# An LSTM with its Wx sums as filler work: steps 16 to 31 by the pair scheme, with factors taken from where they are made

## The chip, the core and the metric

The kernel runs on one core of a Trainium2 chip. Its engines work in parallel, each in the order of its own instruction list: TensorE (PE, matmuls), VectorE (DVE), ScalarE (ACT), GpSimd (POOL) and SyncE (SP), which here only issues transfers. The metric is the device time of one execution in microseconds, the median of several runs. The profile is of one execution; its span is shorter than that execution's time by what lies before the first and behind the last instruction.

## What is computed

The reference is an LSTM over 512 time steps with a residual: batch 32, input and hidden size 512, all in float32.

```
xW = einsum('ntd,dg->ntg', x, Wx) + b
def step((h, c), xw_t):
    a = xw_t + h @ Wh                       # 4 x 512 columns: i, f, o, g
    i, f, o = sigmoid(...);  g = tanh(...)
    c = f * c + i * g
    h = o * tanh(c)
out = x + hs
```

The steps depend on each other. xW of a step depends on nothing but x and Wx, and has to be there before that step.

## The kernel before

**Two kinds of work on TensorE.** For every step k, h_part (L881) multiplies the transposed h by Wh: 32 matmuls onto PSUM banks that already hold xW of that step. Then the cell (L912 to L930) goes through ACT (sigmoid, tanh) and DVE (f·c, i·g, their sum, o·tanh c, the transpose to ht). While TensorE would wait for ht, it does filler work: a part of the Wx sums of later steps. The program is written out window by window: window v holds step k = v − OFF, and whatever products, sums and transfers the tables put there. Windows below OFF have no step, only the Wx sums with which step 0 can start.

**The Wx sums.** x is taken in rows of 8 steps. xW of a row goes by one of these ways:

- *Units* (UNITS, L91): one row and one quarter j of the columns, 7 products of Strassen's kind (s = 1 to 7), each over two blocks k: 56 matmuls of 128x32 by 128x256 a unit, four units a row. A job is one unit; it begins in window job.w and its products are spread over five windows by products(v) (L590): s1, s5 and s6 early, s7 two windows later, s2 and s3 three, s4 four.
- *The pair scheme* (PAIR, L267): two rows together by 14 outer products of 28 matmuls each, with sums of x blocks ("nodes", L512, and s0 to s3, L540 to L543) on the left side, sums of Wx blocks ("factors") on the right, and sums of the results afterwards (L760, L776).
- *The cycle scheme* (CYCLE): four rows by 26 outer products, thirteen times; it begins at window START and carries steps 48 to 495. The last two rows go by units and by direct products.

PAIR_ROW = 4: rows 0 to 3 (steps 0 to 31) are 16 units, rows 4 and 5 (steps 32 to 47) one pair. OFF is 11, so that step 0 stands in window 11.

**What a product leaves.** The first products of a job add up in an "acc" bank, s5 in "p". ACT copies them out (copy_first, copy_fifth, L633 to L639), DVE adds acc and p to pu (L620, "pu_n" for job n), ACT puts pu and acc into the "pp" banks (L627, L628), and DVE adds acc and p again into pp (L629). On these sums the later products pile up: s7 overwrites acc and so waits for L620 of its job; s4 adds into the bank that L629 fills. evacuate(v) (L606) writes these out for one window.

**Factors.** A factor is four strips of Wx sums, of 256, 512, 512 and 512 columns, in two tiles from rings: wa (3 buffers) with the A part (768 columns) and wb (4 buffers) with the B part (1024). push_factors (L405) queues all of them as DVE additions (L418) to be done where there is room; keep (L384) stores each in DRAM by SP, and fetch (L1133) loads the factor that a product needs two windows ahead, also by SP. t_pair (L355, the lines L358 to L360) and t_sums make the sums of Wx blocks (tt_sb) on DVE from which units and factors are formed.

**Other engines.** ACT seeds the step's PSUM banks with xW (L870, L876) and fills xw with the bias (L843). POOL loads xW of step k + 3 from DRAM with an adding transfer (load_xw, L847), and adds x to h for the output (L988): one 128x128 sum a step. SP loads Wh (load_wh, L352, four transfers), rows of x (load_row, L317), the residual rows, and stores xW (L659), factors and output.

Of the kernel before, what the change touches and what calls it, by code (L numbers as in the profile page):

```python
# [14 lines left out]
P = 128  # L15
B = 32
# [52 lines left out]
FACTORS_FROM = 6  # L69
# [20 lines left out]
PAIR_ROW = 4  # L90
# [77 lines left out]
PAIR_SPAN = 18  # L168
START = PAIR_AT + PAIR_SPAN
START_STEP = HEAD - LEAD  # L170
OFF = START - START_STEP
# [3 lines left out]
def pair_begin(n):  # L175

    return n + n * (PAIR_SPAN - PAIRS) // PAIRS

# [14 lines left out]
LOAD_AT = (4, 10, 12)  # L193
WH_AT = (2, 3, 4, 5)
# [62 lines left out]
class Run:  # L257
# [20 lines left out]
def kernel(  # L278
# [124 lines left out]
    factors_left = []  # L403

    def push_factors():  # L405
        v = nc.vector
        made, ops, done = {}, [], []

        def source(u, part):
            if u < 8:  # L410
                return parts_of(u)[part]
            a, b = made[u - 8]
            return (a[:, 0:1], a[:, 1:3], b[:, 0:2], b[:, 2:4])[part]

        def outer(n, how, a, b, part):
            if n not in made:
                made[n] = ring(n, f"make_{n}")
            (v.tensor_add if how == "add" else v.tensor_sub)(source(8 + n, part), source(a, part), source(b, part))  # L418

        for op in B_OPS:  # L420
            if isinstance(op, int):
                n = -1 - op
                ops.append((0, lambda n=n: keep(n, made[n])))
            else:
                for part, columns in enumerate((C, 2 * C, 2 * C, 2 * C)):
                    ops.append((columns, lambda op=op, part=part: outer(*op, part)))
        for n in range(R):
            if streamed(n) and len(B_OF[n]) == 1:
                ops.append((0, lambda i=B_OF[n][0][0], n=n: keep(n, parts_of(i))))
        for i, (columns, fn) in enumerate(ops):  # L430

            def go(fn=fn, i=i):
                fn()
                done.append(fn)
                factors_left.append(len(ops) - 1 - i)

            at = FACTORS_FROM + min(i / 5, 5 + (i - 25) / 12)
            push(at, columns, go, lambda v, i=i, at=at: len(done) == i and v >= at - 1)


# [149 lines left out]
    def products(v):  # L590
        for late, ss in ((4, (4,)), (2, (7,)), (0, (1,)), (1, (6,)), (0, (5,)), (1, (5,)), (3, (2, 3))):
            job = jobs.get(v - late)
            for s in ss if job and job.w < LATE_AT[0] else ():
                if job.w < EARLY and s not in (4, 7):
                    continue
                if s != 5 or job.w5 == v:
                    product(job, s)
                if s == 4:
                    job.release()
        for late, parts in enumerate(LATE_PLAN):  # L600
            job = jobs.get(v - late)
            for s, part in parts if job and job.w >= LATE_AT[0] else ():
                product(job, s, part)
                given[0] += 1

    def evacuate(v, room):  # L606
        taken = run_due(v - 0.5, FIRST_SUMS if room else 0)
        for half, late in ((1, 5), (0, 4)):
            job = jobs.get(v - late)
            if job:  # L610
                taken += job.finish(half)
# [7 lines left out]
        if job and job.w >= EARLY:  # L619
            nc.vector.tensor_add(job.pu[:, 1], job.acc, job.p5)  # L620
            taken += C + FIXED
        job = jobs.get(v - 3)
        if job:
            if room:
                taken += run_due(v, min(room - taken, BETWEEN))
            if job.w >= EARLY:
                nc.scalar.copy(job.pp[0], job.pu)  # L627
            nc.scalar.copy(job.pp[1][:, 0], job.acc)  # L628
            nc.vector.tensor_add(job.pp[1][:, 1], job.acc, job.p5)  # L629
            taken += C + FIXED  # L630
        return taken
# [13 lines left out]
    unit_free = spare + [pair.rearrange("p m t e b -> p m (t e b)") for pair in node_pairs[3:]]  # L645
    others = [t for i in range(8) if i not in RESIDENT for t in (raw[i], tt_[i])]

    def head_done():
        free.extend(t.rearrange("p (h n) c -> p h (n c)", h=2) for t in others)
        free.extend(spare)  # L650
        free.extend(spool.tile([P, 2, 2 * C], F32, name=f"slot_h{i}", tag="sums", bufs=2) for i in range(2))
        node_free.extend(pair[:, e] for pair in node_pairs[3:] for e in range(2))
# [52 lines left out]
    def slot(sb, v):  # L705
        ends = last_use(sb, v)
        if ends:
            sums[sb, v] = sums[sb, ends[0]]
            moved.add((sb, ends[0]))
        else:  # L710
            sums[sb, v] = free.pop(0)
        left_uses[sb, v] = sb.scheme.uses[v]

    def used(sb, v):
        if (sb, v) in left_uses:
            left_uses[sb, v] -= 1
            if left_uses[sb, v] == 0:
                f = sums.pop((sb, v))
                if (sb, v) not in moved:
                    free.append(f)  # L720
# [19 lines left out]
    def finish_product(job, sb, n):  # L740
        c = sb.scheme

        def finish(half):
# [24 lines left out]
            for v in c.by_ready[n]:  # L768
# [4 lines left out]
                def go(v=v):  # L773
# [12 lines left out]
                    and (last_use(sb, v) or len(free) > (at < sb.at + c.limit[v] - 0.5)),  # L786
# [31 lines left out]
    tail_banks = accs[(LATE_AT[0] + 1) % 2], pps[(2 * (len(UNITS) + PAIRS + R * NSB) + 2) % 3]  # L818
# [59 lines left out]
    state = {"c": c_init, "ht": h_init}  # L878
# [236 lines left out]
    def describe(job, sb, n):  # L1115
# [4 lines left out]
        job.kept = None if n < RAW_FIRST and sb.scheme is PAIR else kept.get(factor)  # L1120
        if job.kept is None:
# [11 lines left out]
    def fetch(v):  # L1133

        job = jobs.get(v + 2)
        if job and LATE_AT[0] > job.w >= PAIR_AT and job.kept:
            job.ring = [rpool.tile([P, 3, C], F32, name=f"wa_{job.w}", tag="wa", bufs=3), None]
# [15 lines left out]
        if v in WH_AT:  # L1153
            load_wh(WH_AT.index(v))
# [5 lines left out]
    with tc.manual_schedule():  # L1160
# [45 lines left out]
        for v in range(EARLY, OFF):  # L1206
            if v == NJ + 1:
                push_factors()
# [8 lines left out]
            evacuate(v, 0)  # L1217
# [13 lines left out]
        for k in range(T):  # L1231
# [77 lines left out]
```

## Time and profile before

| What | Value |
|---|---|
| median of 3 runs | 3077.12 us (3077.05 to 3077.36) |
| the profiled execution | 3077.34 us |
| its span | 3075.5 us |
| TensorE busy | 3067.8 us in 56,680 records |
| VectorE, ScalarE, GpSimd busy | 2277.3, 1993.6 and 815.0 us |
| granted TensorE clock | 1.00 |

A float32 matmul of the program leaves two records in the profile, so a product of 4 or 8 matmuls is 8 or 16 records. PE is the matmul, PEld the loading of its weights, which runs beside it. A row of the timeline gives start, duration, engine, line, operation, output and inputs, and in brackets how long the engine had been idle and what ended that. Durations of operations that follow each other overlap a little; the distance from start to start is what one costs in a queue. Line numbers are those of the kernel before.

### The profile page before, as it was taken

The page shows a single profiled execution, that of the slowest core. Times are in us where ns is not written, and L with a number is a line of the kernel's source. Part 1 is how long each engine was busy: PE and PEld are TensorE (multiplying, and loading weights), DVE is VectorE, ACT ScalarE, POOL GpSimd, SP SyncE. Part 2 cuts the span into 40 slices and gives each one's busy share as a digit, 9 for nine tenths or more (in the row PEclk, how much of TensorE's full clock was granted, in tenths as well). Part 3 has the DMA queues.
Part 4 walks back from the last instruction along what each step waited for, and adds up shares of the span by engine and source line. Part 5 has one row for each costly group of instructions (what it writes and reads, how often), then busy time and mean ns, then how long its engine had stood idle before and what let it go on. Part 6 is the DMA issues. An engine that isn't in the chain of part 4 may idle for free.

```text
span 3075.5 us, 133929 instructions
## 1 busy us (share of the span) xinstructions
PE 3067.8 (100%) x56680; PEld 2024.6 (66%) x56680; DVE 2277.3 (74%) x6441; ACT 1993.6 (65%) x5754; POOL 815.0 (26%) x1021
## 2 busy tenths in 40 slices
PE   9999999999999999999999999999999999999999
PEld 5566666666666666666666666666666666666666
DVE  5766777777777777777777777777777777777754
ACT  4566666666666666666666666766666666666665
POOL 0222222222222222222222222222222222222331
PEclk9999999999999999999999999999999999999999
DMA  8988898888889889898988988889898898988753
GB/s 298 301 258 216 228 254 218 254 227 237 241 212 266 226 240 241 211 265 212 261 222 216 270 219 250 226 219 263 218 260 224 227 256 219 258 225 220 196 118 72
DMA packets 343527, 710.71 MB, mean 231 GB/s; under 512 B 45456, under 2 KB 111504, under 8 KB 342416
## 3 DMA queue, kind: packets, MB, share of 16 engines
q1 hardware_dynamic: 269344, 568.41, 56.2%
q0 software_dynamic: 73152, 133.20, 27.2%
q8 instruction: 446, 7.31, 1.0%
q14 instruction: 153, 1.25, 0.1%
q10 hardware_dynamic: 432, 0.53, 0.1%
HBM read 515.97 MB, written 185.99 MB: 228 GB/s over the span
## 4 chain that ended last, share of the span: by engine, by line
PE 99%; DVE 1%; DMA 0%; ACT 0%; issue 0%; SPq 0%; DVEq 0%
PE gates L885 53%; PE acc L581 18%; PE pp L581 18%; PE p L581 6%; PE gates L899 4%; PE pp L802 0%; PE acc L802 0%; DMA raw_sb<-in_L_cond_Wx_dram 0%; PE gates L581 0%; DVE raw_sb L776 0%; DVE c L952 0%; DVE fc L956 0%; DVE fc L950 0%; DVE ht L960 0%; DVE nodes L366 0%
## 5 line engine op out<-in xcount | busy, mean ns | idle before, releaser
L885 PE MATMUL gates<-wh_sb,ht 128*32 128x384 f32 (+1 forms) x30144 | 1725.5, 379 | 0.0
L885 PEld LDWEIGHTS gates<-wh_sb,ht 128*32 128x32 f32 x30144 | 1045.7, 110 | 681.9 <-issue 607.0
L988 POOL TENSOR_TENSOR oc<-xr,ht 128x128 f32<-128x128 f32 x509 | 383.0, 752 | 2162.0 <-DVE ht L930 1959.3
L847 POOL DMA_DIRECT2D xw<-xw x508 | 446.7, 880 | 82.0 <-DMA xw<-nodes 54.4
L922 ACT ACTIVATE s<-gates 128x256 f32<-128x256 f32 x472 | 181.3, 384 | 350.4 <-PE gates L885 339.3
L843 ACT COPY xw<-bias_sb 128x512 f32<-128x512 f32 x508 | 320.9, 632 | 2.0 <-DVE bias_sb L1210 2.0
L581 PE MATMUL pp<-wb,nodes 128*32 128x256 f32 x3920 | 314.7, 379 | 0.0
L925 DVE TENSOR_TENSOR fc<-s,c 128x128 f32<-128x128 f32 x471 | 137.0, 291 | 186.1 <-ACT s L922 183.1
L627 ACT COPY pp<-pu 128x512 f32<-128x512 f32 x398 | 240.0, 603 | 52.7 <-DVE tt_sb L760 21.5
L629 DVE TENSOR_TENSOR pp<-acc,p 128x256 f32<-128x256 f32 x400 | 170.9, 427 | 136.9 <-ACT pp L628 136.7
L929 DVE TENSOR_TENSOR fc<-s,ig 128x128 f32<-128x128 f32 x472 | 137.8, 292 | 177.5 <-ACT ig L928 177.5
L924 ACT ACTIVATE s<-gates 128x128 f32<-128x128 f32 x472 | 131.0, 278 | 147.2 <-PE gates L885 147.2
L870 ACT COPY gates<-xw 128x384 f32<-128x384 f32 x472 | 223.2, 473 | 3.8 <-DMA xw<-xw 3.6
L581 PE MATMUL pp<-wb,s 128*32 128x256 f32 x2656 | 213.2, 379 | 0.0
L581 PE MATMUL acc<-wb,s 128*32 128x256 f32 x2656 | 213.2, 379 | 0.0
L581 PE MATMUL p<-wa,s 128*32 128x256 f32 x2656 | 213.2, 379 | 0.0
L581 PE MATMUL acc<-wa,s 128*32 128x256 f32 x2656 | 213.2, 379 | 0.0
L928 ACT ACTIVATE ig<-c 128x128 f32<-128x128 f32 x472 | 146.3, 310 | 99.3 <-DVE c L927 60.8
L628 ACT COPY pp<-acc 128x256 f32<-128x256 f32 x400 | 144.9, 362 | 87.0 <-DVE tt_sb L760 35.3
L620 DVE TENSOR_TENSOR pu<-acc,p 128x256 f32<-128x256 f32 x398 | 165.2, 415 | 36.8 <-ACT p L639 35.6
L930 DVE STREAM_TRANSPOSE ht<-fc 128x128 f32<-128x128 f32 x472 | 147.0, 312 | 50.7 <-DVE fc L929 1.8
L639 ACT COPY p<-p 128x256 f32<-128x256 f32 x400 | 152.0, 380 | 38.9 <-PE p L581 36.6
(284 smaller groups left out, 4528.3 us busy)
## 6 DMA issues: line engine op xcount, KB each, us to landing
wb<-keep_b SPq DMA_DIRECT2D x332, 512.0 KB, 6.1
xw<-xw POOLq DMA_DIRECT2D x508, 256.0 KB, 5.7
wa<-keep_a SPq DMA_DIRECT2D x332, 384.0 KB, 5.3
xw<-tt_sb SPq DMA_DIRECT2D x420, 128.0 KB, 4.0
xw<-raw_sb SPq DMA_DIRECT2D x288, 128.0 KB, 3.9
xr<-in_x_dram SPq DMA_DIRECT2D x256, 128.0 KB, 5.5
out_dram<-oc SPq DMA_DIRECT2D x255, 128.0 KB, 4.4
row<-in_x_dram SPq DMA_DIRECT2D x63, 512.0 KB, 8.4
```

What stands on the lines that cost most here:

```text
L581: nc.tensor.matmul(dst[t * B : (t + 1) * B], a[:, t % a.shape[1]], w[t // a.shape[1]] if isinstance(w, list) else w, start=(s in (1, 5) or ...
L620: nc.vector.tensor_add(job.pu[:, 1], job.acc, job.p5)
L627: nc.scalar.copy(job.pp[0], job.pu)
L629: nc.vector.tensor_add(job.pp[1][:, 1], job.acc, job.p5)
L639: nc.scalar.copy(job.p5, p5[:, job.w if job.w < EARLY else 0])
L843: nc.scalar.copy(xw[t], bias_sb)
L847: nc.gpsimd.dma_start(out=xw[t], in_=stored[i][a], accum_op=mybir.AluOpType.add)
L870: nc.scalar.copy(gates[t % 2][:, 0:IFG], xw[t][:, 0:IFG])
L885: nc.tensor.matmul(g[j * B : (j + 1) * B, cols], state["ht"][:, k, :], wh_sb[:, k, j, cols], start=False, stop=True, skip_group_check=True,)
L922: nc.scalar.activation(s[:, 0:2], g[:, 0:2], AF.Sigmoid)
L930: nc.vector.transpose(ht.rearrange("p q b -> p (q b)"), h)
L988: (nc.gpsimd if t < T - 3 else nc.vector).tensor_add(state["oc"][:, tt % 2], xr[t][:, tt % 2], ht)
```

## The change

Rows 2 and 3 (steps 16 to 31) no longer go by eight units but by a pair of their own. So there are 8 units (windows 0 to 7), FIRST_PAIR for rows 2 and 3 in windows 8 to 21, SECOND_PAIR for rows 4 and 5 in windows 22 to 37, and the cycles from window 39. OFF becomes 16: step 0 stands in window 16; the cycles still begin at step 23.

The first pair doesn't fetch its factors. Its first four products use Wx blocks as they lie in SBUF, the others the ring tiles in which a factor was just made (make_for_pair). Who makes a factor is divided: POOL (nc.gpsimd) makes 12, 14 and 11 whole, the chain 4+6, −5, −7, −2, +1 (factors 3, 10, 23), the A parts of 7 and 2, the B parts of all products' factors from 7 on, and later 4, 0 and 20; DVE makes 6, 21, 8, 25 and the A parts of 16, 15, 17 and 18. All are still stored for the later fetches. head(v) says in which window each is written. load_xw(0) to load_xw(2) move from the end of the first windows to window 11. In the windows without a step, evacuate_at_first takes the place of evacuate, and products go in the order AT_FIRST: s4, s2, s3, s7, s1, s6, s5. In a step's window load_xw(k + 3) now stands ahead of fetch, in which the POOL additions of a B part are written. Row 3 is loaded in window 2 instead of 4, and Wh one quarter a window from window 2 as before.

What moves, engine by engine. DVE in windows 3 to 5: "pu" is the sum of L620, "nodes_0" a node sum for the first pair, "early_0" the tile pair of factor 6. Before:

```order
L359 TENSOR_TENSOR tt_sb_94<-raw_sb_93,tt_sb_94 128x2x256
L360 TENSOR_TENSOR tt_sb_94<-raw_sb_93,tt_sb_94 128x2x256
L686 TENSOR_TENSOR slot_165<-gates_0_81,pu_0_205 128x512
L620 TENSOR_TENSOR pu_3_364<-acc_1_84,p5_3_366 128x256
L629 TENSOR_TENSOR pp_2_88<-acc_0_83,p5_2_324 128x256
```

After:

```order
L648 TENSOR_TENSOR nodes_0_160<-row_2_112 128x512
L777 TENSOR_TENSOR pu_2_337<-acc_0_83,p5_2_339 128x256
L787 TENSOR_TENSOR pp_0_86<-acc_1_84,p5_1_274 128x256
L369 TENSOR_TENSOR tt_sb_94<-raw_sb_93,tt_sb_94 128x2x256
L370 TENSOR_TENSOR tt_sb_94<-raw_sb_93,tt_sb_94 128x2x256
L843 TENSOR_TENSOR slot_165<-gates_0_81,pu_0_205 128x512
L648 TENSOR_TENSOR nodes_0_160<-row_3_333 128x512
L423 TENSOR_TENSOR wa_early_0_295<-raw_sb_93 128x256
L423 TENSOR_TENSOR wa_early_0_295<-tt_sb_94 128x512
L423 TENSOR_TENSOR wb_early_0_296<-tt_sb_94 128x512
L423 TENSOR_TENSOR wb_early_0_296<-raw_sb_93 128x512
L777 TENSOR_TENSOR pu_3_393<-acc_1_84,p5_3_395 128x256
```

Two node sums and the four strips of early_0 now stand in front of pu_3, the sum that s7 of job 3 waits for.

POOL from the start of the program (behind its constants). Before, where "xw" are the loads of the first steps and "oc" an output sum:

```order
L847 DMA xw_0_493<-xw_0_418 128x512
L847 DMA xw_1_495<-xw_0_418 128x512
L847 DMA xw_2_497<-xw_0_418 128x512
L847 DMA xw_3_499<-xw_0_418 128x512
L988 ISA
L988 TENSOR_TENSOR oc_0_1035<-xr_0_116,ht_0_1025 128x128
```

After:

```order
L423 ISA
L423 TENSOR_TENSOR wa_make_12_299<-raw_sb_93 128x256
L423 TENSOR_TENSOR wa_make_12_299<-tt_sb_94 128x512
L423 TENSOR_TENSOR wb_make_12_302<-tt_sb_94 128x512
L423 TENSOR_TENSOR wb_make_12_302<-raw_sb_93 128x512
L423 TENSOR_TENSOR scratch_1_381<-raw_sb_93 128x256
L423 TENSOR_TENSOR scratch_1_381<-tt_sb_94 128x512
L423 TENSOR_TENSOR scratch_0_380<-tt_sb_94 128x512
L423 TENSOR_TENSOR scratch_0_380<-raw_sb_93 128x512
L423 TENSOR_TENSOR wa_early_1_297<-scratch_1_381,raw_sb_93 128x256
```

Eight whole factors, 32 additions, now stand ahead of the first load of xw.

POOL in the first steps, before:

```order
L988 TENSOR_TENSOR oc_0_1035<-xr_0_116,ht_1_1168 128x128
L847 DMA xw_5_1163<-xw_0_418 128x512
L988 TENSOR_TENSOR oc_2_1315<-xr_2_905,ht_2_1305 128x128
L847 DMA xw_6_1300<-xw_0_418 128x512
L988 TENSOR_TENSOR oc_2_1315<-xr_2_905,ht_3_1445 128x128
```

After:

```order
L423 TENSOR_TENSOR wb_make_16_1382<-tt_sb_94 128x512
L423 TENSOR_TENSOR wb_make_16_1382<-raw_sb_93 128x512
L1145 TENSOR_TENSOR oc_0_1292<-xr_0_116,ht_1_1390 128x128
L1004 DMA xw_5_1385<-xw_0_455 128x512
L423 TENSOR_TENSOR wb_make_15_1495<-tt_sb_94,wb_make_16_1382 128x512
L423 TENSOR_TENSOR wb_make_15_1495<-raw_sb_93,wb_make_16_1382 128x512
L1145 TENSOR_TENSOR oc_2_1513<-xr_2_1182,ht_2_1503 128x128
```

The two strips of a B part now stand ahead of each step's output sum.

The diff, cut to its core:

```diff
-FACTORS_FROM = 6
...
-PAIR_ROW = 4
+PAIR_ROW = 2
...
-PAIR_SPAN = 18
-START = PAIR_AT + PAIR_SPAN
+SECOND_AT = PAIR_AT + PAIRS
+OFF = 16
 START_STEP = HEAD - LEAD
-OFF = START - START_STEP
+START = START_STEP + OFF
...
+def second_begin(n):
+
+    return n + n * (START - SECOND_AT - PAIRS) // PAIRS
...
-LOAD_AT = (4, 10, 12)
-WH_AT = (2, 3, 4, 5)
+LOAD_AT = (2, 14, 15)
+WH_AT = {k: 2 + k for k in range(NJ)}
+KEPT_AT = (11, 4, 12)
+XW_AT = 11
+MADE_AHEAD, ON_POOL = 3, 5
+MAKES_AT = {2: (1, 2), 9: (0, 1), 10: (2, PAIRS - RAW_FIRST - 1)}
...
-PAIR = Scheme(
-    2, PAIR_A_OPS, PAIR_A_OF, PAIR_B, PAIR_C_OPS, PAIR_C_OF, pair_begin, lambda n: False, (), PAIR_SLACK
+FIRST_PAIR, SECOND_PAIR = (
+    Scheme(2, PAIR_A_OPS, PAIR_A_OF, PAIR_B, PAIR_C_OPS, PAIR_C_OF, begin, lambda n: False, (), slack)
+    for begin, slack in ((lambda n: n, [2, 2]), (second_begin, PAIR_SLACK))
 )
-RUNS = [Run(PAIR, PAIR_AT, PAIR_ROW)] + [Run(CYCLE, START + PER * sb, HEAD // ROW + MO * sb) for sb in range(NSB)]
+RUNS = [Run(FIRST_PAIR, PAIR_AT, PAIR_ROW), Run(SECOND_PAIR, SECOND_AT, PAIR_ROW + 2)] + [
+    Run(CYCLE, START + PER * sb, HEAD // ROW + MO * sb) for sb in range(NSB)
+]
+
+
+AT_FIRST = ((4, (4,)), (3, (2, 3)), (2, (7,)), (0, (1,)), (1, (6,)), (0, (5,)))
+IN_STEPS = ((4, (4,)), (2, (7,)), (0, (1,)), (1, (6,)), (0, (5,)), (1, (5,)), (3, (2, 3)))
 
 
...
+    def combine(engine, to, how, a, b, parts):
+        for part in parts:
+            fn = engine.tensor_add if how == "add" else engine.tensor_sub
+            fn(sources(to)[part], sources(a)[part], sources(b)[part])
+
...
+    def make_for_pair(m, n, how, a, b):
+        job = jobs[PAIR_AT + RAW_FIRST + m]
+        assert n == B_AT[PAIR_B[RAW_FIRST + m]]
+
+        def go():
+            job.ring = pair_factors[n] = [rpool.tile([P, 3, C], F32, name=f"wa_make_{n}", tag="wa", bufs=3), None]
+            combine(nc.gpsimd if m < ON_POOL else nc.vector, job.ring, how, a(), b(), A_PART)
+            waiting.append((0 if m >= MADE_AHEAD else KEPT_AT[m], n, job.ring, 0))
+
+        def rest():
+            job.ring[1] = rpool.tile([P, 4, C], F32, name=f"wb_make_{n}", tag="wb", bufs=4)
+            combine(nc.gpsimd, job.ring, how, a(), b(), B_PART)
+            waiting.append((0 if m >= MADE_AHEAD else KEPT_AT[m], n, job.ring, 1))
+
+        if m < MADE_AHEAD:
+            go()
+            rest()
+        elif m < ON_POOL:
+            job.first, job.rest = go, rest
+        else:
+            job.rest = rest
+            push(
+                job.w - 0.5,
+                3 * C + FIXED,
+                go,
+                lambda _: state["window"] >= job.w - 1 and len(pair_factors) == m,
+            )
+
...
+    PAIR_MAKES = (
+        (14, "sub", one(3), one(7)),
+        (12, "sub", one(4), one(0)),
+        (11, "sub", one(0), one(7)),
+        (7, "sub", one(4), one(7)),
+        (2, "sub", one(3), one(0)),
+        (16, "sub", one(2), one(6)),
+        (15, "sub", one(1), made_for(16)),
+        (17, "sub", made_for(15), one(5)),
+        (18, "sub", one(2), one(1)),
+    )
+
+    def head(v):
...
+        if v == 2:
+            rows[PAIR_ROW + 2] = xpool.tile([P, ROW, NJ, B], F32, name=f"row_{PAIR_ROW + 2}", tag="row")
+            unit_free.append(rows[PAIR_ROW + 2].rearrange("p (h t) q b -> p h (t q b)", h=2))
+            scratch.extend(ring(None, name) for name in ("early_0", "early_1"))
+        if v == 4:
+            tiles = [scratch_tile(i) for i in range(2)]
+            extra.append(tiles[0].rearrange("p (h c) -> p h c", h=2))
+            late.append(tiles[1])
+            scratch.append(scratch_set(tiles[1], tiles[0]))
+            make_now(pool, scratch[2], "add", 4, 6)
+            make_now(pool, scratch[1], "sub", scratch[2], 5)
+            make_soon(4, scratch[0], "add", 1, 3, 6)
+            make_soon(6, scratch[2], "sub", scratch[0], 7, 21)
+            make_soon(7, scratch[0], "add", scratch[0], scratch[1], 8)
+            make_soon(8, scratch[2], "sub", 5, scratch[2], 25)
+        if v == 5:
+            keep_now(3, scratch[2])
+            make_now(pool, scratch[1], "sub", scratch[1], 7)
+        if v == 6:
+            keep_now(10, scratch[1])
+        if v == 9:
+            make_now(pool, scratch[1], "sub", scratch[1], 2)
+            make_now(pool, scratch[1], "add", scratch[1], 1)
+        if v == 10:
+            keep_now(23, scratch[1])
+        if v in MAKES_AT:
+            lo, hi = MAKES_AT[v]
+            for m in range(lo, hi):
+                make_for_pair(m, *PAIR_MAKES[m])
...
+        if v == SECOND_AT - 2:
+            scratch[:] = [scratch_set(late[0], scratch_tile(2))]
+            make_now(pool, scratch[0], "add", 0, 6, 4)
+        if v == SECOND_AT:
+            make_now(pool, scratch[0], "add", 2, 3, 0)
...
-        for late, ss in ((4, (4,)), (2, (7,)), (0, (1,)), (1, (6,)), (0, (5,)), (1, (5,)), (3, (2, 3))):
+        for late, ss in AT_FIRST if v < OFF else IN_STEPS:
...
+    def evacuate_at_first(v):
+        finish_halves(v)
+        second_sum(v)
+        third_sum(v)
+        job = jobs.get(v - 1)
+        if job and job.w >= EARLY:
+            copy_first(job)
+            copy_fifth(job)
+
...
-        job.kept = None if n < RAW_FIRST and sb.scheme is PAIR else kept.get(factor)
-        if job.kept is None:
+        job.factor, job.kept = factor, kept.get(factor)
+        if sb.scheme is FIRST_PAIR or sb.scheme is SECOND_PAIR and n == 0:
+            job.kept = None
+        if job.kept is None and n >= RAW_FIRST and sb.scheme is FIRST_PAIR and n < PAIRS - 1:
+            right = lambda s: job.ring[PLACE[s][0]][:, PLACE[s][1]]
+        elif job.kept is None:
             right = lambda s: raw_factor(B_OF[factor][0][0], s)
         else:
...
+        following = jobs.get(v + 1)
+        if following and hasattr(following, "first"):
+            following.first()
+        if job and hasattr(job, "rest"):
+            job.rest()
...
-            if v == NJ + 1:
-                push_factors()
+            head(v)
             if v == NJ + 2:
                 nc.vector.transpose(
                     bias_sb.rearrange("p (m l) -> p m l", l=B),
                 for t in range(4):
                     fill_bias(t)
             announce(v)
-            evacuate(v, 0)
+            if v == XW_AT:
+                for t in range(3):
+                    load_xw(t)
+            run_due(v + 1, 0)
+            evacuate_at_first(v)
             for op in prepare(v):
                 op()
             for op in more[: NJ + EARLY - v - (v == EARLY)]:
                 more.pop(0)()
-            run_due(v, FILL_ROOM)
+            run_due(v + 1, FILL_ROOM if v < PAIR_AT else 0)
             products(v)
             fetch(v)
-        for t in range(3):
-            load_xw(t)
         seed_first(0)
...
-            if v == PAIR_AT + RAW_FIRST - 1:
-                assert factors_left[-1] == 0
-            if v == PAIR_AT + 4:
-                head_done()
+            if v < START:
+                head(v)
             announce(v)
             for op in prepare(v):
                 op()
             run_due(v, room - evacuate(v, room))
             products(v)
             tail_products(v)
-            fetch(v)
             if k + 3 < LATE_END:
                 load_xw(k + 3)
+            fetch(v)
```

More of the change, by code (lines that the diff above doesn't have):

```diff
@@ L401, in ring @@
         )
[L403 to L438, printed above, removed]
@@ new lines, with scratch_tile, scratch_set, keep_now @@
+    scratch = []
+    def scratch_tile(i):
+        return xpool.tile([P, ROW, NJ, B], F32, name=f"scratch_{i}", tag="row").rearrange("p t q b -> p (t q b)")
+    def scratch_set(a, b):
+        return a.rearrange("p (n c) -> p n c", c=C)[:, 0:3], b.rearrange("p (n c) -> p n c", c=C)
+    late, stored_sums, waiting = [], set(), []
+    def keep_now(n, t):
+        keep(n, sources(t) if isinstance(t, int) else t)
+        stored_sums.update((n, half) for half in range(2))
+    def make_now(engine, t, how, a, b, n=None):
+        combine(engine, t, how, a, b, WHOLE)
+        if n is not None:
+            keep_now(n, t)
@@ L607, in evacuate @@
         taken = run_due(v - 0.5, FIRST_SUMS if room else 0)
[L608 to L611, printed above, removed]
+        taken += finish_halves(v)
         job = jobs.get(v - 1)
@@ L644, with as_slot @@
     free = []
[L645 to L652, printed above, removed]
+    pair_slots = [pair.rearrange("p m t e b -> p m (t e b)") for pair in node_pairs[3:]]
+    unit_free = spare + pair_slots
+    pair_free, extra = [], []
+    for run in RUNS:
+        run.pool = pair_free if run.scheme is FIRST_PAIR else free
+    def as_slot(t):
+        return t.rearrange("p (h n) c -> p h (n c)", h=2)
     def store(i, j, f):
@@ L710, in slot @@
         else:
-            sums[sb, v] = free.pop(0)
+            sums[sb, v] = sb.pool.pop(0)
         left_uses[sb, v] = sb.scheme.uses[v]
@@ L719, in used @@
                 if (sb, v) not in moved:
-                    free.append(f)
+                    sb.pool.append(f)
     def put_out(sb, v):
@@ L1136, in fetch @@
         if job and LATE_AT[0] > job.w >= PAIR_AT and job.kept:
+            assert {(job.factor, 0), (job.factor, 1)} <= stored_sums, (v, job.factor)
             job.ring = [rpool.tile([P, 3, C], F32, name=f"wa_{job.w}", tag="wa", bufs=3), None]
```

107 lines of the change are left out of this document (88 added, 19 removed).

## The prediction, made before the changed kernel ran

> **What bounds the kernel now.** I read the page's share of busy time first, then the chain of work that ended last, then who makes TensorE wait.
>
> ```profile
> PE 3067.8 (100%) x56680; PEld 2024.6 (66%) x56680; DVE 2277.3 (74%) x6441; ACT 1993.6 (65%) x5754; POOL 815.0 (26%) x1021
> PE 99%; DVE 1%; DMA 0%; ACT 0%; issue 0%; SPq 0%; DVEq 0%
> ```
>
> TensorE is both the busiest engine and the chain. The waits of PE over the whole span are three rows (line, what it waited for: us in total, times, longest):
>
> ```profile
> PE gates L899 <- DVE fc L950: 1.5, 2, 1.2
> PE pp L1166 <- DVE c_init L338: 1.1, 1, 1.1
> PE gates L581 <- DMA raw_sb<-in_L_cond_Wx_dram: 0.2, 1, 0.2
> ```
>
> So 2.8 us of 3075.5 are idle, and none of it lies where the change works. The time can fall only by fewer products, or by small stalls that the pipelined records hide. The chain from 25 to 60 us, in order of time, shows some of those:
>
> ```profile
> 24.86 0.86 PE p L581 x16
> ...
> 26.59 2.59 PE acc L581 x48
> ...
> 32.63 2.76 PE acc L581 x48
> ...
> 51.24 2.75 PE acc L581 x48
> ```
>
> Forty-eight records cost 2.59 us in an undisturbed piece and 2.75 in the pieces from 32.63 on, one per window; the waits below count five. What the weight loads (PEld) wait for between 30 and 62 us names the reason:
>
> ```profile
> PEld acc L581 <- DVE pp L629: 2.2, 5, 0.4
> ```
>
> A profiled execution of 3077.34 us (1.84 around its span) stands 0.22 above the median of 3077.12; I sum against the profiled one and subtract 0.22 at the end. About 0.2%, 6.2 us, is what a measurement of this kernel can tell from no change: below 3070.97 is faster, above 3083.27 slower.
>
> **Fewer products.** Sixteen units of 56 matmuls and one pair of 14 × 28 become eight units and two pairs: 896 + 392 against 448 + 784, 56 matmuls fewer, 112 records. Sixteen records take 0.864 us (a third of the 2.59 above), 54.0 ns each: **−6.0 us**, all on the path, since TensorE is the path.
>
> **The order of the first windows.** s4, s2 and s3 now stand ahead of s7, and the sum L629 that releases s4 stands ahead of the spare DVE work: the five pieces lose 0.16 each, **−0.8 us**. Floor: 3077.34 − 6.84 = 3070.5, on the median's scale 3070.3.
>
> **Step 0 is not sooner in time against this kernel.** Counting products ahead of step 0's first h matmul, 155 stand there instead of 128, 74.4 us of TensorE against 62.8; steps from 23 on come 6 us earlier. As TensorE is full, when step 0 begins is worth nothing by itself.
>
> **Factors on GpSimd.** Before, all sums of Wx were DVE's (L418). Now POOL makes many of them in 128x512 adds, which the trace doesn't show on POOL. Its only adds are of 128x128 (ns min/median/max):
>
> ```profile
> L988 POOL TENSOR_TENSOR oc<-xr,ht x509: 446/800/1535, 70.1 to 3058.7; 128x128 f32<-128x128 f32 x170
> 1032.07 0.45 POOL L988 TENSOR_TENSOR oc<-xr,ht 128x128 f32<-128x128 f32 x1 [3.94 <-DVE ht L930]
> 1008.30 1.34 POOL L988 TENSOR_TENSOR oc<-xr,ht 128x128 f32<-128x128 f32 x1 [4.81 <-DVE ht L930]
> 1008.14 1.18 DVE L776 TENSOR_TENSOR raw_sb<-raw_sb 128x1024 f32<-128x1024 f32 x1
> ```
>
> The same add takes 0.45 when alone and 1.34 when a 1.18 us DVE sum of two SBUF tensors started just before it: it waits for that sum to end. The reverse, DVE and POOL from 77 us:
>
> ```profile
> 77.31 0.65 DVE L418 TENSOR_TENSOR wa_make<-tt_sb 128x512 f32<-128x512 f32 x1
> 77.88 0.95 DVE L418 TENSOR_TENSOR wb_make<-tt_sb 128x512 f32<-128x512 f32 x1
> 78.75 0.68 DVE L418 TENSOR_TENSOR wb_make<-raw_sb 128x512 f32<-128x512 f32 x1
> 77.48 0.80 POOL L988 TENSOR_TENSOR oc<-xr,ht 128x128 f32<-128x128 f32 x1 [5.95 <-DVE ht L930]
> ```
>
> POOL waits behind the first sum, goes between it and the second, and the second is 0.95 instead of 0.68: a POOL add of 128 columns holds DVE up for 0.27 us. Scaled by columns, 0.54 for 256 and 1.08 for 512, 3.8 us for a factor (256 + 3 × 512). Bounds: at DVE's own pace (below) 0.60 per 512; at the 0.45 per 128 columns of a POOL add alone, 1.8 per 512, 6.3 a factor; below, no hold at all. I take 1.08, being measured as a hold.
>
> [...]
>
> **The early head (S1).** In window 5 TensorE reaches s7 of job 3 at 25.72 + 3 × 0.864 = 28.3 us (window 4 ends with the 24.86 piece). It overwrites the bank that DVE's sum pu_3 reads. DVE from 18 us, before:
>
> ```profile
> 18.70 0.43 DVE L629 TENSOR_TENSOR pp<-acc,p 128x256 f32<-128x256 f32 x1 [1.18 <-ACT pp L628]
> ...
> 22.15 0.43 DVE L629 TENSOR_TENSOR pp<-acc,p 128x256 f32<-128x256 f32 x1 [0.23 <-ACT pp L628]
> 22.49 0.68 DVE L359 TENSOR_TENSOR tt_sb<-raw_sb,tt_sb 128x512 f32<-128x512 f32 x1
> 23.21 0.69 DVE L360 TENSOR_TENSOR tt_sb<-raw_sb,tt_sb 128x512 f32<-128x512 f32 x1
> 23.82 0.68 DVE L686 TENSOR_TENSOR slot<-gates,pu 128x512 f32<-128x512 f32 x1
> 24.93 0.42 DVE L620 TENSOR_TENSOR pu<-acc,p 128x256 f32<-128x256 f32 x1 [0.42 <-PE acc L581]
> 26.96 0.43 DVE L629 TENSOR_TENSOR pp<-acc,p 128x256 f32<-128x256 f32 x1 [1.61 <-ACT pp L628]
> 27.30 0.68 DVE L686 TENSOR_TENSOR nodes<-gates,pu 128x512 f32<-128x512 f32 x1
> ```
>
> Start to start, 512 columns cost 0.60 and 256 0.34. Six sums now stand in front of pu_3: two node sums (2 × 0.60), of which one goes into the waits at 22.15 and 24.93, and the factor early_0 (0.34 + 3 × 0.60). From 24.4, the end of L686, that is 0.60 + 2.14 + 0.34 for pu_3 itself, plus about 0.5 that the waits don't hold: 28.0, just in time. But POOL starts as soon as the first Wx blocks are there, about 11 us, waiting for nothing else: make_12, 4+6, −5 and half of −7 are 14 adds, 3 × 3.8 + 1.6 = 13.0 us of holds. Some cost nothing: those in DVE's waits (the 1.18, 0.23 and 0.42 above and another half microsecond, 2.3 in all) and beside sums that read PSUM (about 1.6). The other 9.1 push pu_3 to about 37: **S1 = 9 us**. At 0.60 per 512 it is 7.3 − 3.9 − 0.3 = 3; with no hold 0; at 1.8 some 17.
>
> **Steps 0 to 5 (S2).** POOL now makes half (the B part, 2 × 512) of one factor in each of five step windows, released by TensorE's s4 just behind the h matmuls, the time of the cell. One step of before, DVE and then PE:
>
> ```profile
> 150.45 0.29 DVE L925 TENSOR_TENSOR fc<-s,c 128x128 f32<-128x128 f32 x1 [1.18 <-ACT s L922]
> ...
> 151.64 0.29 DVE L929 TENSOR_TENSOR fc<-s,ig 128x128 f32<-128x128 f32 x1 [0.37 <-ACT ig L928]
> 152.04 0.31 DVE L930 STREAM_TRANSPOSE ht<-fc 128x128 f32<-128x128 f32 x1
> 147.20 3.64 PE L885 MATMUL gates<-wh_sb,ht 128*32 128x384 f32 x64
> 153.25 1.47 PE L885 MATMUL gates<-wh_sb,ht 128*32 128x384 f32 x16
> ```
>
> The four sums and products of the cell (L925 to L929) read two SBUF tensors each, and take 1.9 us with the transpose. A window of step 0 to 5 is 3.46 of h and seven half-size products of 0.43, 6.48 us; DVE's list there (factor parts, three or four output sums, five small sums) is 4.2 to 4.4, with the cell 6.2 to 6.4: 0.1 to 0.3 to spare. The holds are 2 × 1.08 + 0.27 = 2.4 us a window; I take half of them to fall beside work that doesn't contend (PSUM sums, the transpose, ACT's tanh) and so 1.2 − 0.2 = 1.0 on the path: **S2 = 5 us**; none to 2.2 each, 0 to 11.
>
> **Other edits.** The fetches that the first pair saves lie on SP's queue, which TensorE never waits for. Row 3 is now loaded behind one Wh load instead of three, and DVE's second node sum waits for it; the transfers, KB each and us to land:
>
> ```profile
> wh_sb<-in_L_cond_Wh_dram SPq DMA_DIRECT2D x4, 1024.0 KB, 11.0
> 11.84 3.81 SPq L353 DMA_DIRECT2D wh_sb<-in_L_cond_Wh_dram  x3
> ```
>
> The first Wh load lands at 11.84 + 11.0 = 22.8 and row 3, half its size in the same queue, some 1.5 later, 24.3: before the node sum at 25, so nothing; if it were 2 us late, pu_3 would be late by that much, inside S1 where the holds delay it anyway. In a step window POOL's list is B part, output sum (waits for ht), load_xw of three steps on: 2.2 + 0.8 + 0.9 of 6.5 us, and the load has 18 us to land, so what queues behind the waiting sum costs nothing. Behind POOL's eight factors stand load_xw(0) to (2), which feed the seeds of step 0: 11.1 + 8 × 4.5 (1.08 + 0.18 of overhead an add) + some 0.35 of waiting on each of 32 adds (0.80 − 0.45), with a store of 5 us to land in between, about 71; these rows say the rest:
>
> ```profile
> xw<-xw POOLq DMA_DIRECT2D x508, 256.0 KB, 5.7
> L847 POOL DMA_DIRECT2D xw<-xw x508 | 446.7, 880 | 82.0 <-DMA xw<-nodes 54.4
> ```
>
> 0.9 to issue, 5.7 to land: 78, for a step 0 that S1 has put off to 74.4 + 9 = 83. In time, by 5 us.
>
> **Sum.** 3077.34 − 6.0 − 0.8 + 9 + 5 − 0.22 = 3084.3; I say 3084.
>
> **The rivals.**
> *A, no lasting collision.* If POOL's adds slip into DVE's waits, S1 and S2 are under 0.7: 3070.3 to 3071, faster. For it: 26% of POOL and 26% of DVE are free. Against: 0.95 and 1.34, and a DVE list with 0.3 us to spare at 28.3. It decides if pu_3 ends by 28.9. Chance 0.10, 0.08 of it below the bound.
> *B, one stall only.* Holds at DVE's pace, or steps that hide theirs: S1 3 to 9 and S2 0 to 3, 3073 to 3082, no change. Chance 0.25.
> *C, the POOL chain is the bound.* At 6.3 us a factor load_xw(0) lands at about 93, against 73.6 for the seeds of an unstalled step 0: 3070.3 + 19.4 = 3089.7, and S2 on top up to 3096. It decides from about 5.7 us a factor. For it: 0.45 alone for 128 columns; against: the 0.27. Chance 0.10, slower.
> *Forecast*, both stalls at the measured hold: chance 0.55, of which 0.40 above 3083.3 and 0.15 below; its own range 3079 to 3091 (S1 7 to 11, S2 2 to 10).
> Faster 0.08; slower 0.40 + 0.10 = 0.50; same 0.42. The range from 3070.5, A's end, to 3091 leaves out about 1 in 10, most of it C's upper half.
>
> **What would show it.** Right: a row of PE or PEld waiting for DVE's pu sum near 28 us, for several us; POOL adds of 128x512 above 1.1 us; DVE sums of 128x512 near 1.7 from 11 to 37 us; PE waits for ht in steps 0 to 5 of about 1 us. Wrong: no wait of PE before 60 us (S1 falls, A or B), sums of 0.65 beside POOL's adds (no hold), or a wait of step 0 for xw (C).

## The result and the profile after

The changed kernel took 3101.55 us (median of 6 runs, 3099.45 to 3103.06) against 3077.35 of the kernel before (6 runs, 3077.05 to 3077.44): ratio 1.0078, 95% interval 1.0066 to 1.0091, 24 us slower. That lies outside the range that the prediction gave. The direction and the mechanism named in it hold; its size does not. The profiled execution is one of 3102.48 us.

The page's busy times and the chain of the changed kernel:

```profile
PE 3071.9 (99%) x56568; PEld 2026.8 (65%) x56568; DVE 2322.5 (75%) x6479; ACT 2001.7 (65%) x5770; POOL 897.7 (29%) x1085
PE 95%; DVE 2%; issue 1%; POOL 0%; ACT 0%; DMA 0%; DVEq 0%; POOLq 0%
```

112 records fewer, as counted, and yet 4 us more of busy TensorE: some matmuls ran slowly. The chain is no longer TensorE alone. Who it waits for, over the span (line, releaser: us in total, times, longest):

```profile
PE acc L717 <- DVE pp L787: 8.6, 5, 4.4
PE acc L717 <- DVE pu L777: 8.2, 4, 4.2
PE gates L1042 <- DVE ht L1087: 2.4, 2, 1.8
```

L777 and L787 are the sums of acc and p (L620 and L629 before), L1087 the transpose to ht. All three releasers are on VectorE. TensorE's busy time by stretch (from:to us, length, busy and records, granted clock, DMA share, GB/s):

```profile
0.00:20.00 20.00, 17.31 (x248) 1.00 0.93 350
20.00:36.00 16.00, 10.00 (x184) 0.97 0.76 307
36.00:42.00 6.00, 5.75 (x56) 0.52 0.88 214
42.00:64.00 22.00, 20.90 (x388) 1.00 0.79 282
64.00:84.00 20.00, 20.00 (x378) 1.00 0.96 281
84.00:94.00 10.00, 6.76 (x124) 0.95 0.83 275
94.00:100.00 6.00, 5.96 (x52) 0.51 0.98 281
100.00:131.00 31.00, 23.82 (x436) 0.99 0.57 177
131.00:137.60 6.60, 5.92 (x52) 0.52 0.98 287
137.60:200.00 62.40, 60.99 (x1124) 1.00 0.79 221
```

The kernel before is idle for 1.3 us in its first 20 and not at all from 20 to 200. Here the idle parts add up to 22.6 us: 1.4 more than before up to 20, 7.4 from 20 to 64, 12.5 from 84 to 200. And in three stretches the clock is about 0.5: some 5.6 us each, from 36.2, 94.0 and 131.7, in which TensorE does half the work, 2.8 us lost each, 8.5 together. Each of them follows one of the three longest waits (4.17, 2.43 and 4.39 us). 21.3 + 8.5 is 30 of the 31 us that stand between 3102.5 and the 3071.3 that the fewer products alone would leave of 3077.34.

The first stall is the one that was forecast. VectorE, GpSimd and TensorE of the changed kernel:

```profile
31.30 1.76 DVE L423 TENSOR_TENSOR wa_early<-tt_sb 128x512 f32<-128x512 f32 x1
32.98 1.21 DVE L423 TENSOR_TENSOR wb_early<-tt_sb 128x512 f32<-128x512 f32 x1
34.11 1.74 DVE L423 TENSOR_TENSOR wb_early<-raw_sb 128x512 f32<-128x512 f32 x1
35.78 0.41 DVE L777 TENSOR_TENSOR pu<-acc,p 128x256 f32<-128x256 f32 x1
31.06 1.45 POOL L423 TENSOR_TENSOR wb_early<-scratch,raw_sb 128x512 f32<-128x512 f32 x1
32.48 1.17 POOL L423 TENSOR_TENSOR wa_early<-wa_early,raw_sb 128x256 f32<-128x256 f32 x1
33.60 1.71 POOL L423 TENSOR_TENSOR wa_early<-wa_early,tt_sb 128x512 f32<-128x512 f32 x1
36.25 1.08 PE L717 MATMUL acc<-tt_sb,s_h 128*32 128x256 f32 x8 [4.17 <-DVE pu L777]
```

The two engines take turns. A VectorE sum of 128x512 shows 1.76 us where one alone shows 0.68: the 1.08 more is GpSimd's turn of 512 columns; behind a 256-column turn (32.48) it shows 1.21, 0.53 more. The sum pu_3 starts at 35.78, and TensorE goes on at 36.25. It had waited 2.08 us for pu_2 at 25.83 already, so the last wait is 4.17 and not the whole delay.

In steps 0 and 4 the same turns fall on short sums. VectorE in both, with the wait that follows, and GpSimd in step 4:

```profile
90.41 2.63 DVE L679 TENSOR_TENSOR s<-nodes,s 128x128 f32<-128x128 f32 x1
94.04 1.08 PE L717 MATMUL acc<-wa_make,s 128*32 128x256 f32 x8 [2.43 <-DVE pp L787]
125.27 1.37 DVE L676 TENSOR_TENSOR s<-nodes 128x128 f32<-128x128 f32 x1
126.56 1.35 DVE L679 TENSOR_TENSOR s<-nodes,s 128x128 f32<-128x128 f32 x1
127.84 3.44 DVE L678 TENSOR_TENSOR s<-row 128x128 f32<-128x128 f32 x1
131.68 1.08 PE L717 MATMUL acc<-wa_make,s 128*32 128x256 f32 x8 [4.39 <-DVE pp L787]
127.71 0.90 POOL L1004 DMA_DIRECT2D xw<-xw  x1
128.33 1.58 POOL L423 TENSOR_TENSOR wb_make<-tt_sb 128x512 f32<-128x512 f32 x1
129.56 1.56 POOL L423 TENSOR_TENSOR wb_make<-raw_sb 128x512 f32<-128x512 f32 x1
```

A sum of 128 columns (0.28 us alone) waits here for one GpSimd sum of 512 (1.37 and 1.35 us), or for more than one (3.44): three of them take 6 us. GpSimd makes factor 4 and a B part there, from 122.8 to 131.1, with one load's issue (L1004) between. The sums of 3.44 and 2.63 us ended only when two GpSimd sums had gone by, and both stand where those two follow directly behind a load's issue (at 127.71, and at 89.46 in step 0). No other VectorE sum of 128 columns in this trace takes over 1.4 us. Why GpSimd goes twice there was not tried.

### The profile page after: what moved, and what is told of

The parts are those of the page before. It is cut to its first block, busy times and chain, and to the rows that moved or that the text cites. A ratio compares the mean times of both kernels' runs of the same rounds, so it can differ in the third digit from the quotient of the medians.

```text
span 3100.7 us, 133856 instructions
## 1 busy us (share of the span) xinstructions
PE 3071.9 (99%) x56568; PEld 2026.8 (65%) x56568; DVE 2322.5 (75%) x6479; ACT 2001.7 (65%) x5770; POOL 897.7 (29%) x1085
## 4 chain that ended last, share of the span: by engine, by line
PE 95%; DVE 2%; issue 1%; POOL 0%; ACT 0%; DMA 0%; DVEq 0%; POOLq 0%
PE gates L1042 52%; PE acc L717 17%; PE pp L717 17%; PE p L717 6%; PE gates L1056 4%; PE acc L959 0%; PE pp L959 0%; DVE wb_early L423 0%; DVE s L677 0%; DVE s L678 0%; POOL wb_make L423 0%; DVE s L679 0%; DVE scratch L423 0%; DVE s L676 0%; DVE pu L777 0%
## 5 line engine op out<-in xcount | busy, mean ns | idle before, releaser
L1004 POOL DMA_DIRECT2D xw<-xw x508 | 447.8, 883 | 23.7 <-ACT gates L1021 3.5
L787 DVE TENSOR_TENSOR pp<-acc,p 128x256 f32<-128x256 f32 x406 | 173.3, 427 | 103.6 <-ACT pp L786 103.4
L777 DVE TENSOR_TENSOR pu<-acc,p 128x256 f32<-128x256 f32 x404 | 167.7, 415 | 47.5 <-ACT p L796 35.1
L1087 DVE STREAM_TRANSPOSE ht<-fc 128x128 f32<-128x128 f32 x472 | 147.0, 311 | 50.3 <-DVE fc L1086 1.4
```

Of the source, the lines that this page charges most:

```text
L1004: nc.gpsimd.dma_start(out=xw[t], in_=stored[i][a], accum_op=mybir.AluOpType.add)
L1087: nc.vector.transpose(ht.rearrange("p q b -> p (q b)"), h)
```

## The experiments

**The early sums, the late ones, and all of them.** In write_all GpSimd fills each strip with a constant, and its sums of Wx blocks are left out; write_head does so in windows below 12 only, write_steps from 12 on.

```diff
         for part in parts:
+            if engine is nc.gpsimd:          # write_head: and state["window"] < 12; write_steps: >= 12
+                engine.memset(sources(to)[part], 0.01)
+                continue
             fn = engine.tensor_add if how == "add" else engine.tensor_sub
```

> The changed kernel, with every GpSimd sum of Wx blocks replaced by a GpSimd fill of the same tile with a constant (so the sums themselves are left out, and nothing of SBUF is read by GpSimd there). The place in GpSimd's list, the tiles, the waits for them and all of VectorE's work stay. Theory, GpSimd's adds hold up VectorE's sums of two SBUF tensors, TensorE then waits and each wait of 2.4 us and more is followed by 5.6 us at half clock: nearly all stalls go, 3070.3 to 3072. Rival, VectorE's own added work (node sums and factor early_0 ahead of pu_3, a full list in steps 0 to 5) makes the stalls: the waits for pu and pp stay, 3090 to 3101.

> As write_all, but only in windows below 12, the eight whole factors ahead of the first load of xw (these sums are left out); the B parts in the steps stay. Theory: the stalls before 64 us go (8.7 us idle and 2.8 of half clock), those from 84 us on stay (12.5 idle and 5.7 of half clock): about 3088. Rival, the early delay causes the later ones: it falls to 3072 or so. Rival, VectorE's own work: 3100.

> As write_all, but only in windows from 12 on: the A and B parts of the first pair and factors 4, 0 and 20 (these sums are left out); the eight early factors stay. Theory: the stalls from 84 us on go, those before 64 stay: 3077.1 - 6.8 + 8.7 + 2.8 = 3081 to 3083. Rival, the steps are late for their full VectorE list: 3095 to 3100.

Measured: write_all 3071.51 us (ratio to before 0.9982, 0.9973 to 0.9991), write_head 3089.06 (1.0040, 1.0026 to 1.0054), write_steps 3081.37 (1.0014, 1.0005 to 1.0023). All three came out as the theory had it. VectorE's own added work alone makes no stall. (The fills wait for no input and run much earlier than the sums did; write_long, below, keeps the wait for the inputs.) The early sums cost 9.9 us (3081.37 − 3071.51), the later ones 17.6 (3089.06 − 3071.51), and 2.6 of the 30 us are left, to be seen only with both, if at all: the runs of the changed kernel are 3.6 us apart among themselves.

**The order of the first windows alone**, put into the kernel before: AT_FIRST, evacuate_at_first and a run_due ahead of it.

> The kernel before, with the order of products (s4, s2, s3, s7, s1, s6, s5) and of evacuations of the changed kernel in the windows without a step, and nothing else. Theory: the five losses of 0.16 us in windows 6 to 10 go: 0.8 us less, 3076.5. Rival: the loss moves to another product of the window, within 0.2 of 3077.3.

Measured: 3077.00 us against 3077.13, ratio 0.9999 (0.9990 to 1.0008), no change that can be told, and not the 0.8 of the theory. The five pieces are 2.59 us now, as the chain of this kernel shows, and TensorE is busy for 0.7 us less (3067.1). But it is idle for 0.4 more, with a new wait of 0.3 at h matmuls, and the span (3075.2) is only 0.3 us shorter:

```profile
34.23 2.59 PE acc L581 x48
...
40.27 2.59 PE acc L581 x48
```

```profile
PE gates L906 <- ACT pp L629: 0.3, 1, 0.3
```

**What halves the clock.** The kernel before, with waits of growing length put ahead of the transpose in cell.

```diff
         nc.vector.tensor_mul(h, s[:, 3], tc_t)
+        for _ in range((t - 60) // 28 + 2 if t >= 60 and (t - 60) % 28 == 0 else 0):
+            nc.vector.tensor_mul(s[:, 0:2], s[:, 0:2], s[:, 0:2])
```

> The kernel before, with 2, 3, 4 up to 16 further VectorE products of 128x256 (on a tile that nothing reads any more, 0.46 us each) ahead of the transpose of steps 60, 88, 116 up to 452, so that TensorE waits for ht from about 0.3 to 6.5 us in fifteen places. The clock granted behind each tells from which idle time on it is halved. Theory: waits up to about 2.2 us cost their own length, those above about 2.4 to 4 are followed by some 5.6 us at half clock, 2.8 us more each. Rival: the half clock in the changed kernel came from something else (its transfers, its load), and every wait here costs its own length alone, at clock 1.00.

Measured: 3147.01 us in one run, which is read for its clock alone. TensorE's first matmuls behind some of the waits (idle time in the brackets), and the 6 us that follow each, with the granted clock behind the bracket of records:

```profile
1282.20 3.66 PE L885 MATMUL gates<-wh_sb,ht 128*32 128x384 f32 x64 [1.96 <-DVE ht L932]
1450.66 6.60 PE L885 MATMUL gates<-wh_sb,ht 128*32 128x384 f32 x64 [2.92 <-DVE ht L932]
1622.45 3.66 PE L885 MATMUL gates<-wh_sb,ht 128*32 128x384 f32 x64 [3.31 <-DVE ht L932]
1791.89 4.96 PE L885 MATMUL gates<-wh_sb,ht 128*32 128x384 f32 x64 [3.47 <-DVE ht L932]
```

```profile
1282.20:1288.20 6.00, 6.00 (x112) 1.00 0.35 64
1450.66:1456.66 6.00, 6.00 (x52) 0.50 0.53 116
1622.45:1628.45 6.00, 6.00 (x112) 1.00 0.32 46
1791.89:1797.89 6.00, 6.00 (x88) 0.78 0.69 148
```

The waits up to 1.96 us left the clock at 1.00; 2.92 halved it, 3.31 did not, and all seven from 3.47 to 6.61 did. Nothing of the change is in this kernel, so the rival is out: a wait alone brings the half clock. Other runs widen the band. A wait of 2.43 (the changed kernel, step 0), of 2.44 (whole_late) and of 2.00 (dve_all) was followed by half clock; one of 2.08 (the changed kernel, at 25.83) and the same 2.00 in dve_head were not. So between 2.0 and 3.4 us the length alone does not settle it, and the theory's edge between 2.2 and 2.4 is not one. Nor do its 5.6 us hold: read in half-microsecond slices, the halved time is about 3.4 or 6.8 us long (here 3.4 behind the waits of 3.47 and 4.70, 6.8 behind the six others), part of it in the wait itself (in the changed kernel 6.8 each time, of which 1.0 to 1.3 in the wait). What sets the two lengths no run here shows.

**Which of the later sums.** b_parts keeps on GpSimd only the B parts of 16, 15, 17 and 18 (steps 1 to 4), whole_late only factors 7 and 2 around step 0, the B part of 2 among them, and 4, 0 and 20 behind; all others are fills.

```diff
+            state["b_part"] = m >= ON_POOL
             combine(nc.gpsimd, job.ring, how, a(), b(), B_PART)
+            state["b_part"] = False
```

> As write_all (sums of Wx blocks on GpSimd replaced by fills, left out), but the B parts of factors 16, 15, 17 and 18, two sums of 128x512 in each of four step windows, stay on GpSimd. That is the term that the prediction priced at 1.0 us a window. Theory, the term was right and the rest of the steps' loss came from whole factors that it did not price: 3071.5 + 4 = 3075 to 3077. Rival, the B parts alone make the waits of 4.4 us and the half clock: 3082 or more.

> The reverse of b_parts in windows from 12 on: factors 7 and 2 (both parts) around step 0 and factors 4, 0 and 20 stay on GpSimd, the B parts of 16, 15, 17, 18 and the eight early factors are filled (left out). Theory: eight sums in a row at 82 to 93 us and five at 123 to 128 make TensorE wait 2 to 3 us once or twice and halve the clock: 3071.5 + 6 to 12 = 3078 to 3084. Rival: these land in idle time of VectorE, 3072 to 3073, and it is the B parts.

Measured: b_parts 3077.30 us (0.9999, 0.9990 to 1.0009), 5.8 above write_all; whole_late 3079.57 (1.0007, 0.9998 to 1.0017), 8.1 above. whole_late lies in its range, b_parts 0.3 above, and neither rival fits: both terms stand, and the one of whole factors, which the prediction did not price, is the larger. TensorE's waits in b_parts, then in whole_late:

```profile
88.42 3.66 PE L1047 MATMUL gates<-wh_sb,ht 128*32 128x384 f32 x64 [1.57 <-ACT gates L1038]
96.87 3.66 PE L1047 MATMUL gates<-wh_sb,ht 128*32 128x384 f32 x64 [1.77 <-ACT gates L1038]
105.40 3.66 PE L1047 MATMUL gates<-wh_sb,ht 128*32 128x384 f32 x64 [1.85 <-DVE ht L1092]
112.88 3.66 PE L1047 MATMUL gates<-wh_sb,ht 128*32 128x384 f32 x64 [0.80 <-DVE ht L1092]
```

```profile
78.46 0.64 PE L722 MATMUL acc<-wb_make,s 128*32 128x256 f32 x8 [0.84 <-DVE pu L782]
81.97 1.08 PE L722 MATMUL acc<-wa_make,s 128*32 128x256 f32 x8 [2.44 <-DVE pp L792]
```

Four waits of 0.8 to 1.85, behind which the clock stayed at 1.00, come from the B parts. Eight sums in a row around step 0 make one wait of 2.44 us, and the 1.08 of the eight records behind it (0.64 at full clock) is the halved clock. 5.8 and 8.1 are 13.9 of the 17.6 us of all later sums. The 3.7 left point to step 4: its wait of 4.39 us, with the half clock behind, is in write_head too (4.4 us, and a granted clock of 0.97 from 64 to 200 us), but in b_parts, where factor 4 is filled, TensorE waits 0.80 there, and in whole_late, where the B part behind the load's issue is filled, the product that waited 4.39 us starts at 110.88, 0.3 us late (0.72 behind the start of the one before, against 0.43), and the next h matmuls wait 0.16.

**Reading or writing.** In the changed kernel, each strip on GpSimd is a sum of the first column of every block and two fills of the rest.

```diff
+            if engine is nc.gpsimd:
+                fn(to_[:, :, 0:1], a_[:, :, 0:1], b_[:, :, 0:1])
+                for _ in range(2):
+                    engine.memset(to_[:, :, 1:], 0.01)
+                continue
```

> The changed kernel; in place of each GpSimd sum of a strip one sum of its first column in each block (so that it still waits for its inputs) and two fills of the strip, which write only and take 1.0 us for 512 columns together: the sums are left out, GpSimd is busy as long, at the same places. Theory, what holds VectorE up is that GpSimd reads SBUF: VectorE's sums of 128x512 stay at 0.68 us beside the fills, 3071 to 3073. Rival, any use of SBUF by GpSimd of that length holds: sums of 1.2 to 1.7 us and 3090 or more.

Measured: 3071.10 us (0.9981, 0.9971 to 0.9990), with write_all (3071.51) the least of all versions. GpSimd and VectorE side by side:

```profile
24.60 1.10 POOL L427 MEMSET wa_early<- 128x510 f32 x2
25.67 0.20 POOL L425 TENSOR_TENSOR wb_early<-scratch,tt_sb 128x2 f32<-128x2 f32 x1
25.81 1.10 POOL L427 MEMSET wb_early<- 128x510 f32 x2
24.52 0.69 DVE L430 TENSOR_TENSOR wa_early<-tt_sb 128x512 f32<-128x512 f32 x1
25.13 0.68 DVE L430 TENSOR_TENSOR wb_early<-tt_sb 128x512 f32<-128x512 f32 x1
25.73 0.69 DVE L430 TENSOR_TENSOR wb_early<-raw_sb 128x512 f32<-128x512 f32 x1
```

With GpSimd busy and only writing, VectorE's sums take 0.68 or 0.69, where the one beside GpSimd's sums, at 31.30 in the changed kernel, takes 1.76. It is GpSimd's reading that holds them.

**The same sums on VectorE.** dve_steps moves those from window 12 on, at their place; dve_head the eight early factors, strip by strip into VectorE's idle time; dve_all both.

```diff
+        if state["window"] >= 12:            # dve_steps, dve_all
+            engine = nc.vector
...
+            push((10 if i < 20 else 12 if i < 44 else 13) + i / 100,   # dve_head, dve_all
+                 (C, 2 * C, 2 * C, 2 * C)[part], go, lambda _, i=i: len(strips_done) == i)
```

> The changed kernel with the sums of Wx blocks of windows from 12 on made by VectorE at the same places of the program (0.60 us for 512 columns instead of 1.08 of hold). Theory: VectorE's list of 6.3 of 6.48 us takes 1.2 us more in each of five step windows, about 1 us of wait each, too short for the clock: 3081.4 + 5 = 3086 to 3089. Rival: what counts is that VectorE's list is full, whoever adds to it: 3100 or more.

> The changed kernel with the eight whole factors of windows below 12 made by VectorE, strip by strip, where its list has idle time (windows 5 to 13, factor 14 ahead of 12), GpSimd only from window 12 on. Theory: VectorE has some 28 of 74 us free there for 20 us of sums, so the stalls before 64 us go as in write_head: 3089 to 3092. Rival: VectorE has no room and the stalls stay: 3098 or more.

> Both: all sums of Wx blocks on VectorE, the early ones placed in its idle time, those of the steps at their place. Theory: 3071.5 with no stall, 5 us in the steps and 0 to 3 in the head: 3077 to 3080, about the kernel before. Rival: the sums were the load, not the sharing: 3090 or more.

Measured: dve_steps 3094.55 us (1.0058, 1.0043 to 1.0073), dve_head 3092.59 (1.0051, 1.0034 to 1.0068), dve_all 3087.32 (1.0033, 1.0020 to 1.0047). Each is faster than the changed kernel and slower than the theory said: 6 us past its range for dve_steps, 7 for dve_all, 0.6 for dve_head. The rivals don't fit either: all three lie below what they said. TensorE in dve_all, in four stretches:

```profile
0.00:64.00 64.00, 60.09 (x1018) 0.97 0.94 323
64.00:84.00 20.00, 17.74 (x308) 1.00 0.96 329
84.00:134.00 50.00, 43.56 (x788) 1.00 0.77 232
134.00:200.00 66.00, 63.82 (x1167) 1.00 0.85 250
```

From 84 to 134 us 6.4 us are idle where 5 were expected, and 2.2 more behind, around the two sums of factor 20, for which the expectation had no term. The other 3.9 and 2.3 us (1.3 of them as in the kernel before) lie where the strips were put in VectorE's list. In the one place that the next line shows, the transpose of the bias stands behind seven strips in VectorE's list, and ACT, which waits for it, releases TensorE 2.0 us late at 34.65. The 1.89 us of the sixteen records (1.07 in dve_head, at full clock) show half clock; it lasts 3.4 us in this execution, the slowest of the five:

```profile
34.65 1.89 PE L749 MATMUL pp<-raw_sb,row 128*32 128x256 f32 x16 [2.00 <-ACT pp L817]
```

So VectorE's idle time can take the early sums only where nothing else is queued behind them. That a better placing would bring dve_all below the kernel before was not tried: 6.4 us in the steps remain, as much as the 56 matmuls bring.

## Why the prediction was wrong, by its own steps

Two steps failed: S2 left out sums that the change names, and every stall was priced without the slow clock behind it. Of the 17 us between 3084.3 and 3101.55, the profiled execution shows 8.5 as half clock, 7.5 as further waits from 84 us on (12.5 where S2 had 5) and 0.7 as the gain of the order that did not come; about 1 us is not placed.

- **Fewer products, −6.0 us**: right. With GpSimd's reads gone (write_long) the kernel takes 3071.10, 6.1 below the kernel before in the same comparison.
- **The order of the first windows, −0.8 us**: mis-sized. The 0.16 us pieces went, and 0.1 us came of it (before_order); 0.4 us of idle time came in their place, 0.3 of it a wait at the h matmuls.
- **The hold of 1.08 us for 512 columns**: right, and measured (1.76 − 0.68). A GpSimd sum of 512 columns takes 1.27 to 1.28 us alone (at 83.17 and 68.31), against the 1.08 + 0.18 taken. That it comes from reading was not shown before write_long.
- **S1, 9 us**: the place and the sum are right, and nearly the time: pu_3 ends at 36.2, where 37 was forecast. The delay is not one wait, though: 1.4 us more than before are idle in the first 20 us, 2.08 at pu_2, 4.17 at pu_3. Another 1.1 stand between 42 and 64 us, which the sum did not have, so that the total of 8.8 meets the 9 partly by luck. Left out was the half clock behind the wait, 2.8 us.
- **S2, 5 us**: the first step that failed. It priced the B parts of five windows (steps 0 to 4) at 1.0 us each; those of steps 1 to 4 measure 5.8 together (b_parts), 1.45 each, within its bounds. It did not price the rest of factors 7 and 2 around step 0, nor 4, 0 and 20, which stand in the text of the change: with the B part of step 0 they cost 8.1 us alone (whole_late). Together with the step where both kinds meet it is 17.6 (write_head against write_all), the half clock included.
- **That a hold costs what its columns say**: short sums were left out of this. In steps 0 and 4 a sum of 128 columns gave GpSimd a whole turn as a long one does, or two behind a load's issue, so VectorE's list with its short sums was delayed most where it had the least work (1.37, 1.35 and 3.44 us for three sums of 0.28).
- **The clock**: the second step that failed, a term put at nothing. Every stall was priced at its own length, and the longest three cost 2.8 us more each, 8.5 in all. That the trace of before shows no half clock was no reason: its longest wait is 1.2 us.
- **The POOL chain (rival C)**: rightly rejected. No wait of TensorE names the first loads of xw. That they are issued from 72.1 us where 71 was worked out is luck: the terms as they stand (11.1 + 36 + 11.2 + 5) add up to 63, and in the trace GpSimd stands idle for 11.1 us ahead of 49.3, waiting for a VectorE sum, which the working does not have. A and B are out as well: both stalls came, and both cost.

What remains open is what decides between 2.0 and 3.4 us of wait whether the clock is halved, why GpSimd goes twice behind a load's issue, and whether the 2.6 us that the early and the late sums cost only together are more than spread.

## What to carry to other kernels

Before work is handed to an idle GpSimd, look at whether VectorE's operations beside it read two SBUF tensors (in the changed kernel those that read PSUM kept their 0.41 and 0.68 us beside GpSimd's sums, at 25.36 and 88.28): here the work was not moved by that, it took VectorE's time in turns, and more of it (1.08 us for 512 columns) than VectorE would need (0.60). Count every instruction that an engine gets, by its place in the list, and not only those of the regular window. A stall of TensorE is to be priced with the slow matmuls behind it: always from 3.47 us on in these runs, sometimes from 2.0 on.

## What the runs showed of the hardware that was not expected

- A wait of TensorE of 2.92 us was followed by half clock, one of 3.31 was not, and all from 3.47 to 6.61 were; in other runs waits of 2.00, 2.43 and 2.44 us were too, one of 2.08 and another of 2.00 not. The halved time lasts about 3.4 or 6.8 us, at most 1.7 or 3.4 us of work, less what falls into the wait.
- GpSimd's fills of 128x512 take 0.52 us and leave VectorE's sums of 512 columns at 0.68 or 0.69; its sums of two SBUF tensors take 1.27 alone and hold VectorE for 1.08.
- Turns were not always taken one by one: VectorE sums of 128 columns took 2.63 and 3.44 us where two GpSimd sums stood directly behind a load's issue. What let GpSimd go twice there was not tried.
